# One line moved in a slot of the attention loop: ScalarE's exponentials behind the first half of the group work

## The chip, the cores and the metric

The kernel runs on one core of a Trainium2 chip. The metric is the device time of one execution in microseconds (us); a lower figure is better. The five engines are named as in the profile: PE is TensorE's matmuls, PEld its weight loads, DVE is VectorE, ACT is ScalarE, POOL is GpSimd, and SP is the engine that issues most of the DMAs here.

## What is computed

The input is an image batch of 32 x 128 x 56 x 56 in float32. Layer 0 is a depthwise 7x7 convolution, a layer norm and a mixture of experts with eight experts. Layer 1 works on tokens: there are 32 x 3136 = 100352 of them, each with 128 channels. Its attention is unusual, since it looks across the channels of one head of one token rather than across tokens:

```python
qkv = x @ w_qkv + b_qkv                              # x is the normalised token
q, k, v = (to_heads(t) for t in jnp.split(qkv, 3, axis=-1))   # 8 heads of 16
attn = softmax((q * scale)[..., :, None] * k[..., None, :], axis=-1)   # 16 x 16 per head and token
out = jnp.einsum('bhlij,bhlj->bhli', attn, v)
t = t + (out @ w_proj + b_proj)
```

After it comes a second mixture of experts, in which each of 64 experts takes the tokens of an image that score highest for it. The change lies in the attention stage alone.

## The kernel before

The stages follow one another: convolution, routing and experts (up to 4.31 ms of the span), attention (from about 4.33 to 8.86 ms), and the second mixture with the output. In the attention stage 128 tokens make a tile, seven tiles make a group (`GJ = 7`), and there are 784 tiles (`NT`) and 112 groups (`NG`). Seven groups hold a pair of images.

**A tile's work.** A tile has 128 partitions of 16 x 8 x 16 = 2048 scores. `offsets` (DVE) writes key minus pivot into a buffer `s`; `scores` (POOL) multiplies it by the query in place; `exps` (ACT) takes the exponential in place; `values` (DVE) multiplies by the value vector into `ev`. `sums_s` and `sums_ev` (PE) add up the 16 slices of `s` and of `ev` in PSUM by 16 transposing matmuls each. For every second tile `keys` (PE) computes keys and values of two tiles into the PSUM tile `kv`, `ends` (DVE, two reductions named `kx`) finds the largest and the smallest key of each head, `pivots` (POOL) makes the pivot `c` from them, and `inverse_first` (ACT, two instructions named `r`) and `quotients` (DVE) divide. `s` has five buffers, `ev` three, and `kv` three of two tiles each.

**The slot.** The loop at lines 1479 to 1496 is a software pipeline that is written out by hand. Slot `k` calls each step for another tile: `tile_work(k, back, what)` works on tile `k - back`. So a tile's offsets and scores fall in slot n, its exponentials in slot n + 1, its values and `sums_s` in slot n + 2, and its `sums_ev` in slot n + 3. Each engine is wrapped in `InOrder`, which ties every instruction to the one before it on that engine, so each engine's queue has the order of the text.

**The group's work.** What is done once for seven tiles is cut into pieces with a place in half slots, counted from the group's first tile. `group_work(2 * k)` issues the pieces of the first half of a slot (the even places), and `group_work(2 * k + 1)` those of the second half (the odd places):

```python
(-9, head_turned, first), (-8, head_turned, last),
(-6, head_queries, first), (-5, head_queries, last),
(27, tail_summed, first), (28, tail_summed, last),
(30, tail_rows, first), (31, tail_rows, last),
(39, tail_scale, first), (40, tail_scale, last),
(46, tail_turned, first), (49, tail_turned, last),
```

These six kinds (`takes`) are ACT instructions that empty a PSUM bank which PE had filled a slot or so before: `zT<-p_x`, `q<-p_q`, `t<-pp`, `u<-p_u` with squares `sq<-p_u`, `ls<-p_l` and `lg<-p_g`. Squares of the next groups' tokens (`sq<-tr`), their scaling (`zr`) and `root_first` (`st`) are ACT work too. `choose`, the second mixture's choice of tokens for a pair of images, is a generator that group_work moves on by one step each half slot. All its ACT work, the two passes `pb` over 3136 columns and the scalings `mT<-cm`, falls in even places, since it starts at an even one and its steps lie two or eight half slots apart. The banks for all these transposes and products (`p_x`, `p_q`, `pp`, `p_u`, `p_l`, `p_g`, and `cm` and `acc` of `choose`) come from one ring of three PSUM buffers with the tag `tp`. PE can write to one of them only when ACT or DVE has emptied what it held three allocations before.

Of the kernel before, what the change touches and what calls it, by code (L numbers as in the profile page):

```python
# [25 lines left out]
def conv_attn_hybrid_kernel(  # L26
# [392 lines left out]
    with tc.tile_pool(name="sel", bufs=1) as se, tc.tile_pool(  # L419
# [75 lines left out]
        for e in range(E):  # L495
            k = key[:, e, :]
# [456 lines left out]
    def fetch(i):  # L953

        e = slice(i * Q, (i + 1) * Q)
        fw1s[i] = big.tile([C, Q, FF2], F32, name="fw1", tag="s", bufs=5)
        nc.sync.dma_start(fw1s[i], weight1[e, :C, :].rearrange("e c f -> c e f"))
        fw2s[i] = big.tile([P, Q, NF2, C], F32, name="fw2", tag="ev", bufs=3)
        nc.sync.dma_start(fw2s[i], weight2[e, :FF2, :].rearrange("e (p f) o -> p e f o", f=NF2))

    with tc.tile_pool(name="at_c", bufs=1) as cc, tc.tile_pool(
# [503 lines left out]
        def group_work(place):  # L1465
            for what, of in work.pop(place, ()):
                what(*of)
            if place in choices:
                choosing.append(choose(choices.pop(place)))
            if choosing and next(choosing[0], run) is run:  # L1470
                choosing.pop(0)

        def tile_work(k, back, what, every=1):
            n = k - back
            if 0 <= n < NT and n % every == 0:
                what(n)

        k = -22
        while k < NT or work or choosing or choices:
            tile_work(k, 5, inverse_first, 2)  # L1480
            tile_work(k, -1, ends, 2)
            tile_work(k, 6, quotients, 2)
            tile_work(k, 0, offsets)
            tile_work(k, -1, pivots, 2)
            tile_work(k, 0, scores)
            tile_work(k, 1, exps)
            tile_work(k, -2, keys, 2)
            tile_work(k, 3, sums_ev)
            group_work(2 * k)
            tile_work(k, 2, values)  # L1490
            tile_work(k, 2, sums_s)
            group_work(2 * k + 1)
            if k == NT + 4:
                for i in range(3):
                    fetch(i)
            k += 1
# [121 lines left out]
```

## Time and profile before

| | us |
|---|---|
| median of 3 runs (lowest, highest) | 9425.73 (9423.46, 9436.19) |
| the profiled execution's own time | 9417.63 |
| its span in the profile | 9415.9 |
| attention stage in it, 4340 to 8865 | 4525 |
| busy in that stage: DVE / POOL / PE / ACT | 4368 / 4264 / 4298 / 3689 |

A line of a group of instructions reads: line of the kernel, engine, operation, result and operands with their shapes, and the count; then the busy time in us and the mean of one in ns; then how long the engine had been idle just before these instructions, and what ended most of it. Line 161 stands for all attention instructions, since a helper issues them, so they are told apart by their tiles' names. A line of the waits reads: who waited, for what; us in total, number of waits, longest one. A line of the timeline reads: start in us, duration in us, engine, operation, tiles, count, and in brackets the idle time before it and what ended it.

### The profile page before, as it was taken

The numbers are of one execution on the slowest core, as the hardware profiler recorded it, in microseconds if no ns is written. First come the engines' busy times: TensorE is split into PE (matmuls) and PEld (weight loads), VectorE is DVE, ScalarE is ACT, GpSimd is POOL, SyncE is SP. The second block draws the span as 40 slices with busy tenths as digits, with TensorE's granted clock in tenths as the row PEclk, the third lists the DMA queues.
The fourth block names the chain that finished last, engine by engine and source line by source line (L and its number), as shares of the span: only waits on it lengthen the run. The fifth ranks groups of instructions, "written<-read, shape, count | busy, mean of one in ns | idle before, by whom it ended". The sixth has DMA issues, their size and how long they took to land. (4 is left out here: it accounts for less than half of the span.)

```text
span 9415.9 us, 162622 instructions
## 1 busy us (share of the span) xinstructions
PE 8433.8 (90%) x60648; PEld 6763.7 (72%) x60648; DVE 6437.0 (68%) x10943; ACT 5265.5 (56%) x13401; POOL 6911.7 (73%) x5332
## 2 busy tenths in 40 slices
PE   9998278776999999997999999999999999999878
PEld 3436255554666666666888998988889989888733
DVE  2118889883222222226999999999999999999623
ACT  1118724332333333335888888888888888888600
POOL 0007267777777777778999999999999999999500
PEclk9999699998999999999999999999999999999855
DMA  9996157774444444441000000000000000000299
GB/s 210 215 204 179 34 171 225 209 209 121 69 67 72 65 61 70 70 68 32 25 31 32 30 30 32 25 32 32 28 32 32 25 32 30 30 32 32 65 323 335
DMA packets 996135, 849.73 MB, mean 90 GB/s; under 512 B 525012, under 2 KB 880663, under 8 KB 975858
## 3 DMA queue, kind: packets, MB, share of 16 engines
q1 hardware_dynamic: 470162, 494.25, 18.3%
q0 software_dynamic: 177664, 188.81, 11.3%
q10 hardware_dynamic: 347520, 156.28, 6.1%
q8 instruction: 480, 7.86, 0.3%
q14 instruction: 309, 2.53, 0.1%
HBM read 486.34 MB, written 353.64 MB: 89 GB/s over the span
## 5 line engine op out<-in xcount | busy, mean ns | idle before, releaser
L161 POOL TENSOR_TENSOR s<-s,q 128x2048 f32<-128x2048 f32 x784 | 3601.9, 4605 | 136.1 <-DVE s L161 105.5
L161 ACT ACTIVATE s<-s 128x2048 f32<-128x2048 f32 x784 | 1501.0, 1915 | 687.5 <-POOL s L161 684.0
L161 POOL DMA_INDIRECT t_d<-ys,xe x992 | 1530.6, 1543 | 406.1 <-issue 229.6
L161 DVE TENSOR_TENSOR s<-kv,c 128x2048 f32<-128x2048 f32 x784 | 1788.5, 2281 | 8.0 <-POOL c L161 8.0
L161 DVE TENSOR_TENSOR ev<-s,kv 128x2048 f32<-128x2048 f32 x784 | 1785.7, 2278 | 2.4 <-ACT s L161 2.4
L161 PE MATMUL sm<-ident,ev 128*128 128x128 f32 x12544 | 1531.9, 276 | 45.6 <-DVE ev L161 45.6
L161 PE MATMUL sm<-ident,s 128*128 128x128 f32 x12544 | 1526.3, 276 | 8.4 <-ACT s L161 8.4
L161 PEld LDWEIGHTS sm<-ident,ev 128*128 128x128 f32 x12544 | 1437.4, 144 | 92.9 <-DVE ev L161 50.8
L161 PEld LDWEIGHTS sm<-ident,s 128*128 128x128 f32 x12544 | 1404.8, 143 | 21.0 <-ACT s L161 8.9
L907 ACT ACTIVATE hT<-ph,b1t 128x512 f32<-128x512 f32 (+1 forms) x992 | 679.5, 685 | 1236.4 <-PE ph L903 1220.8
L918 DVE TENSOR_TENSOR ys<-py,b2t 128x512 f32<-128x512 f32 (+1 forms) x248 | 171.6, 692 | 1542.2 <-PE py L913 1445.5
L913 PEld LDWEIGHTS py<-w,hT 128*128 128x128 f32 x7936 | 959.3, 192 | 201.9 <-issue 91.4
L903 PE MATMUL ph<-xeT,w 128*128 128x512 f32 (+1 forms) x1984 | 921.6, 597 | 69.7 <-DVE xeT L899 69.7
L913 PE MATMUL py<-w,hT 128*128 128x128 f32 x7936 | 983.5, 278 | 0.2
L716 POOL DMA_INDIRECT xb_d<-xs,rd x784 | 765.3, 976 | 240.7 <-issue 202.0
L241 PE MATMUL cps<-xin,br 56*64 56x448 f32 x7168 | 684.4, 540 | 11.1 <-DVE br L235 10.7
L903 PEld LDWEIGHTS ph<-xeT,w 128*128 128x128 f32 x1984 | 348.7, 191 | 391.9 <-issue 293.1
L241 PEld LDWEIGHTS cps<-xin,br 56*64 56x64 f32 x7168 | 283.5, 132 | 411.2 <-issue 410.0
L161 PE MATMUL pa<-rw,ct 128*128 128x256 f32 x1568 | 395.4, 391 | 157.4 <-DVE xs L161 157.2
L287 POOL MEMSET code<- 128x64 f32 x1 | 0.2, 151 | 691.7 <-DMA conv_d<-ot 691.7
L161 PEld LDWEIGHTS pa<-rw,ct 128*128 128x128 f32 x1568 | 279.3, 191 | 290.8 <-DVE xs L161 209.2
L161 PE MATMUL kv<-wq,zT 128*128 128x256 f32 x1568 | 417.1, 389 | 54.5 <-DVE ev L161 54.1
(558 smaller groups left out, 13031.2 us busy)
## 6 DMA issues: line engine op xcount, KB each, us to landing
ct<-conv_d SPq DMA_DIRECT2D x192, 448.0 KB
xin<-in_x_dram SPq DMA_DIRECT2D x256, 196.0 KB
conv_d<-ot ACTq DMA_DIRECT2D x512, 98.0 KB
t_d<-xs ACTq DMA_DIRECT2D x112, 448.0 KB
tr<-t_d SPq DMA_DIRECT2D x112, 448.0 KB
to<-t_d SPq DMA_DIRECT2D x32, 1568.0 KB
out_dram<-oo ACTq DMA_DIRECT2D x32, 1568.0 KB
xg<-in_x_dram SPq DMA_DIRECT2D x96, 448.0 KB
```

What stands on the lines that cost most here:

```text
L161: r = getattr(self.engine, name)(*a, **k)
L241: nc.tensor.matmul(pss[r][b * HP : (b + 1) * HP], br[rows, kw, :], xi[rows, b * NB : (b + 1) * NB, kw : kw + W], start=(kw == 0), stop=(kw ...
L287: nc.gpsimd.memset(code, -1.0)
L716: s = nc.gpsimd.indirect_dma_start(out=xb_d, out_offset=bass.IndirectOffsetOnAxis(ap=idx, axis=0), in_=row, in_offset=None, bounds_check=R ...
L903: nc.tensor.matmul(ph[:, :, :rows], w1[:, f * P : (f + 1) * P], xT[:, :, :rows], start=True, stop=True,)
L907: nc.scalar.activation(hT[:, f, :, :rows], ph[:, :, :rows], AF.Gelu, bias=b1t[:, f : f + 1])
L913: nc.tensor.matmul(py[:rows, j, :], hT[:, f, j, :rows], w2[:, f, :], start=(f == 0), stop=(f == NF - 1),)
L918: nc.vector.tensor_tensor(ys[:rows], py[:rows], across(b2t, SB)[:rows], ALU.add)
```

## The change

In a slot's text the call of `exps` moves from ahead of `keys`, `sums_ev` and the first `group_work` to directly behind that `group_work`. Nothing is added or removed, and no buffer changes.

```diff
             tile_work(k, 0, scores)
-            tile_work(k, 1, exps)
             tile_work(k, -2, keys, 2)
             tile_work(k, 3, sums_ev)
             group_work(2 * k)
+            tile_work(k, 1, exps)
             tile_work(k, 2, values)
             tile_work(k, 2, sums_s)
             group_work(2 * k + 1)
```

`exps` is one ACT instruction on a tile. `keys` and `sums_ev` issue PE instructions only.

## The prediction

> **What bounds the kernel now.** I first read the busy time by stage, to see which engine leaves least over. The change touches the attention stage only, so this is the stretch from 4340 to 8865 us (columns: length, then busy time of PE, PEld, DVE, ACT, POOL, the granted clock, DMA):
>
> ```profile
> 4340.00:8865.00 4525.00, 4297.62 (x35604) 4061.00 (x35605) 4368.46 (x3816) 3689.26 (x9137) 4264.25 (x2465) 0.98 0.09 30
> ```
>
> DVE is busy for 4368 of 4525 us, 96.5%. What the stage can give is therefore its 157 us of idle time, unless work is taken off DVE, which this change doesn't do. POOL (94%) and PE (95%) are close behind; ACT has 836 us to spare. The next view is the waits of DVE and of PE in 4550 to 8750 us:
>
> ```profile
> DVE kx L161 <- PE kv L161: 95.7, 106, 4.6
> DVE sm L161 <- ACT r L161: 6.3, 14, 1.4
> ...
> PE kv L161 <- DVE ev L161: 52.0, 25, 3.8
> PE sm L161 <- DVE ev L161: 42.4, 21, 3.5
> PE cm L161 <- ACT lg L161: 32.4, 22, 2.8
> PE cm L161 <- ACT sq L161: 16.8, 14, 1.5
> PE acc L161 <- ACT sq L161: 15.3, 19, 2.1
> PE p_x L161 <- ACT sq L161: 11.1, 10, 1.8
> ```
>
> DVE has one wait of any size: keys that PE delivers late. PE's own waits are of two kinds. It waits for DVE where it is ahead, and for ACT to empty a bank. DVE never waits for the exponentials here. ACT waits a great deal, by the page's row of the exponentials:
>
> ```profile
> L161 ACT ACTIVATE s<-s 128x2048 f32<-128x2048 f32 x784 | 1501.0, 1915 | 687.5 <-POOL s L161 684.0
> ```
>
> In 410 of 784 slots ACT stands in front of a tile whose scores POOL hasn't finished, and the bank-emptying behind it stands too. The third view, the timeline, shows the whole chain once:
>
> ```profile
> 6756.54 1.90 ACT L161 ACTIVATE s<-s 128x2048 f32<-128x2048 f32 x1
> ...
> 6758.34 0.57 ACT L161 COPY u<-p_u 128x512 f32<-128x512 f32 x1
> ...
> 6760.00 1.77 PE L161 MATMUL acc<-mT,u 128*128 128x64 f32 x14 [1.03 <-ACT sq L161]
> ...
> 6763.80 1.03 PE L161 MATMUL kv<-wq,zT 128*128 128x256 f32 x4
> ...
> 6764.87 0.76 DVE L161 TENSOR_REDUCE kx<-kv 128x16 f32<-128x256 f32 x2 [1.31 <-PE kv L161]
> ```
>
> ACT takes 1.9 us for exponentials, only then empties `p_u`; PE waits 1.03 us for that bank, is late with the keys 3.8 us later, and DVE stands for 1.31 us.
>
> **What the Trainium skill says.** "PSUM — Partial Sum Buffer", section Engine vs sequencer instructions: the queues of ScalarE, VectorE and GpSimdE are strict FIFO, and matmuls start in program order. The chain above agrees: the copy doesn't pass the exponential. "Perfetto Trace Analysis", Identifying the Most-Contended Engine, warns that PE's matmul busy share is no measure of its limit; so I take DVE as the bound, and PE's 95% only as a warning (it had 220 us of waits in the stage). The same page, Matmuls, wants PSUM banks rotated so that emptying one overlaps the next; here three banks rotate, and the overlap fails where ACT is held up. "ScalarE: Activation LUTs", What ACT_TABLE_LOAD costs, gives 186 ns + 0.833 ns an element without pointer operands, so an estimate of 1892 ns for 2048; the row has 1915 ns. The new neighbours are the same functions, and ACT's rows of this stage hold no table load.
>
> **The change, part by part.** One ACT instruction per tile, 784 in all, changes places with the ACT instructions of the first half of group work. PE's, DVE's, POOL's and SP's queues keep their order: `exps` issues nothing there, no DMA, and the pieces' DMAs stay in sequence. Those behind even pieces (`t2_d`) may start earlier at a DMA share of 0.09, and POOL's `root_step` waits for `root_first`, an even piece that comes earlier: nothing for either. Busy times stay as they are.
>
> *Removed: waits of PE.* From the timeline of ACT I took start-to-start times of the pieces (a square with its accumulator read 0.26 us, `zr` 0.31, `mT` or `ls` 0.22, `u` 0.45, `t` 0.58, a `pb` 2.9) and summed them by the code's places. The first half averages 1.38 us a slot (nine in ten below 2.74, largest 4.1), the second 1.13. I then traced every PE wait of 0.1 us or more for ACT between 4350 and 8840 us to the ACT instruction that ended it. There are 113 waits with 120.7 us, and 119.6 us of them end with an instruction of the **first half**. All of these gain what stands before them, 1.91 us of exponentials plus the wait for POOL, and nearly every wait is shorter than that: 120 us of PE's idle time would go.
>
> *What of it reaches DVE.* Not all, so I kept a ledger along the timeline: a removed PE wait is a credit; a late `kv` at DVE spends from it, up to the length of DVE's wait; a PE wait for DVE's `ev` sets it to zero, since there PE was early anyhow. Of 96.9 us of late keys, **85.3 us** are covered. Both ends: at most all 96.9 plus the 6 us for `r`, about 103; at least nothing, should PE's own work refill the gap.
>
> *Added: later exponentials.* A tile's exponentials now start at the later of two times: the end of POOL's scores, or the end of ACT's earlier work plus the first half's pieces. Against the trace that is 0.92 us later on average, and 1.19 us if ACT also waits for PE to finish the banks that these pieces read (258 us of such waiting, mostly in time in which POOL wasn't done either). Who waits for exponentials? `values` on DVE and `sums_s` on PE, each a slot later. The distance from the end of `exps` to the start of `values` of the same tile is 3.26 us in the median, 1.69 at the fifth percentile. Subtracting tile by tile, 28 tiles would hold DVE back, by **10.0 us** together. Behind the late exponentials stand the second half's pieces and `r`; they end no later than now except where ACT waits for PE, because the same work has only been turned round in front of a wait.
>
> *Slack that the gain itself uses up.* If DVE runs 85 us faster over 784 slots, it gains 0.11 us a slot, 0.22 us over the two slots from offsets to values, and the distance shrinks by that. The same subtraction with all distances 0.5 us shorter gives 44 us in 104 tiles; between 10 and 44, at 0.22, I take **25 us**. The two bounds are 10 us and, with 1 us less, 110 us in 164 tiles; a stall gives the next tiles their slack back, so such a sum is rather too high.
>
> *Ends of the stage.* The last tile's exponentials come one first half later, at most 2 us, and fetches of expert weights wait for its buffers. The gap in PE's clock is nothing that I can price: the granted clock was 0.98 in this stage and 0.5 to 0.6 behind it, where DMA is 0.78 to 0.95 busy.
>
> *Sum*: -85 + 25 = -60 us. The profiled execution took 9417.63 us (span 9415.9), so a like one would take about 9358. The median of the runs shown is 8.1 us higher; against it the forecast is 9425.7 - 60 = **9366 us**. DVE would then be busy for about 4368 of 4465 us, 98%.
>
> **The rivals.** A measurement of this kernel can tell about 0.2%, 19 us, from no change.
>
> *Nothing comes through.* PE gets its banks earlier but then waits for DVE: `kv` and `sm` wait for `ev` for 94 us already in the view above, 46 times. For it: PE has 95% of work, so a removed wait of 1 us may be filled by a queue that was late anyway. Against it: 85 of 97 us of late keys follow a wait for ACT with no wait for DVE in between. A quarter of the 85 would come through, 21 us, against 10 to 25 us of stalls: -11 to +4, about 9422 us.
>
> *Late exponentials take DVE's time* (the slower side). Place: the slots in which the first half is long (`u` with its squares, `lg` with a root step, each with or without seven `mT`) and in which ACT didn't wait for POOL, so that the exponentials move by the full 2 to 2.7 us. Price: with distances shorter by 1 us it is 110 us, net +25; by 1.5 us 216 us in 242 tiles, net +131. It decides from a shortening of about 0.8 us, where stalls and the 85 us cancel. For it: the median distance after the move is only 2.07 us and the fifth percentile 0.06; POOL starts its scores 1.1 us behind DVE's offsets in the median, and would lag more if DVE ran faster. Against it: POOL needs 4264 us for the stage and DVE 4368, so POOL can follow a DVE without waits, and today POOL waits for `s` from DVE 103 us in 106 slots. At a shortening of 1 us it would be about 9450 us.
>
> *More than forecast.* All late keys vanish and stalls stay at 10 us: -93 us, 9333 us.
>
> That the change doesn't do what it says is no likely case: `InOrder` ties ACT's instructions to the text.
>
> **How the numbers follow.** Forecast 0.60, more than forecast 0.08, nothing through 0.14, late exponentials 0.18. Faster by over 0.2% are the first two, 0.68; within it 0.14; slower by over it 0.18. The forecast's own range is 9340 to 9400. The range that should hold 8 in 10 reaches from 9335, beyond which lies half of the strong case, to 9450, which takes in the quiet case and the mild half of the slow one.
>
> **What would show it.** Right: PE's waits for ACT `lg` and `sq` fall from 120 us to under 30, DVE's wait of `kx` for `kv` from 96 to under 30; ACT's wait for POOL before exponentials falls from 684 to under 350 us; a new wait of DVE `ev` for ACT `s` appears, 2.4 us now, 10 to 45 then; the stage ends about 60 us earlier. The forecast is wrong if DVE's wait for `kv` stays above 60 us (the ledger fails: PE's own work was the cause) or if DVE's wait for ACT's `s` passes 85 us (the distance fails).

## The result, and the profile after

The changed kernel takes 9351.6 us (median of 4 runs, 9348.3 to 9354.7) against 9430.1 us of the kernel before beside it: ratio 0.992, interval 0.9907 to 0.9932, so 78 us less. The two profiled executions took 9348.25 and 9417.63 us, 69 us apart.

By the rows of the tile `s`, the attention stage, taken here from the start of the first offsets to the start of the last tile's values, ran from 4334.8 to 8778.7 us:

```profile
L161 DVE TENSOR_TENSOR s<-kv,c x784: 2269/2279/2293, 4334.8 to 8767.6; 128x2048 f32<-128x2048 f32 x196
...
L161 DVE TENSOR_TENSOR ev<-s,kv x784: 2265/2276/2290, 4345.5 to 8778.7; 128x2048 f32<-128x2048 f32 x196
```

That is 4443.9 us, where the kernel before had 4515.9 (4333.9 to 8849.8): 72 us less. All other time went from 4900.0 to 4902.6 us. So the whole difference lies in this stage. The busy times there (length, PE, PEld, DVE, ACT, POOL, clock, DMA share) are nearly what they were, with a DVE that now stands at 98%:

```profile
4335.00:8779.00 4444.00, 4272.11 (x35499) 4034.58 (x35498) 4360.49 (x3812) 3666.99 (x9107) 4263.00 (x2461) 0.99 0.09 30
```

The waits of DVE, then those of PE, in 4550 to 8750 us, the window of the prediction:

```profile
DVE kx L161 <- PE kv L161: 31.6, 51, 1.2
DVE s L161 <- POOL c L161: 9.8, 17, 0.9
DVE ev L161 <- ACT s L161: 1.0, 4, 0.4
```

```profile
PE kv L161 <- DVE ev L161: 52.7, 25, 3.8
PE sm L161 <- DVE ev L161: 47.6, 26, 3.5
PE p_x L161 <- ACT sq L161: 20.9, 27, 1.5
PE p_g L161 <- ACT zT L161: 10.6, 21, 0.8
PE p_g L161 <- ACT sq L161: 9.2, 14, 1.1
```

Late keys fell from 95.7 to 31.6 us. PE's waits for `lg` are gone, and so are all waits of `cm` and `acc`. What PE still waits for from ACT are other banks. The wait for exponentials that DVE was to pay costs it 1.0 us. The timeline of the tile that the prediction showed (before: 6756.54) reads now:

```profile
6719.17 0.57 ACT L161 COPY u<-p_u 128x512 f32<-128x512 f32 x1
...
6721.23 1.92 ACT L161 ACTIVATE s<-s 128x2048 f32<-128x2048 f32 x1
...
6721.47 1.67 PE L161 MATMUL acc<-mT,u 128*128 128x64 f32 x14
...
6725.17 1.03 PE L161 MATMUL kv<-wq,zT 128*128 128x256 f32 x4
...
6727.22 0.74 DVE L161 TENSOR_REDUCE kx<-kv 128x16 f32<-128x256 f32 x2
```

The copy stands ahead of the exponential, `acc` finds its bank empty, and neither PE nor the reduction has a wait in brackets.

### The profile page after: what moved, and what is told of

Same layout as the page of the kernel before. It is cut to its first block, busy times and chain, and to the rows that moved or that the text cites. A ratio compares the mean times of both kernels' runs of the same rounds, so it can differ in the third digit from the quotient of the medians.

```text
span 9346.5 us, 162593 instructions
## 1 busy us (share of the span) xinstructions
PE 8420.5 (90%) x60648; PEld 6741.5 (72%) x60648; DVE 6429.3 (69%) x10943; ACT 5251.3 (56%) x13401; POOL 6907.4 (74%) x5332
## 5 line engine op out<-in xcount | busy, mean ns | idle before, releaser
L161 DVE TENSOR_TENSOR s<-kv,c 128x2048 f32<-128x2048 f32 x784 | 1787.3, 2280 | 20.3 <-POOL c L161 20.2
```

What stands on the lines that cost most here:

```text
L161: r = getattr(self.engine, name)(*a, **k)
```

## The experiments

**Two theories.** The banks theory: PE gets its PSUM banks sooner, so the keys, so DVE. The fill theory: any ACT work done while ACT waits for POOL is worth time, in proportion. For the kernels e1 to e8 the chip spent some 430 us more outside attention than the one of the runs above (before: 9858 to 9861 us), so times are given as ratios to the kernel before beside them, and stages in us. The stages can be compared all the same: the changed kernel's, repeated there as e5, took 4444.0 us, where the first one took 4443.9. The last two ran where the kernel before takes 9424 us.

**The two parts of the first half.** In e1 only the six kinds of `takes` stay ahead of the exponentials; in e2 only the other ACT work does. The division isn't quite that of banks: the scalings `mT<-cm` empty a bank of the ring too, and they belong to the other work.

```diff
-            group_work(2 * k)
+            takes_work(2 * k)          # e1: `takes`; e2 has rest_work(2 * k) here: squares of tr, zr, roots, choose's ACT steps
             tile_work(k, 1, exps)
+            group_work(2 * k)          # what is left of the half
```

> Only the pieces of the first half that empty a PSUM bank (zT, q, t, u with its squares, ls, lg; about 0.53 us a slot) stay ahead of the exponentials; the other squares, the scaling, the root steps and all of the token choice's ACT work (0.85 us a slot) go behind them again. Banks theory (the gain comes from PE getting its banks sooner, and so the keys): the whole gain is kept, 9340 to 9365 us, PE's waits for ACT stay under 60 us and DVE's wait for kv near 30 us. Fill theory (any ACT work done in the wait for POOL brings gain, in proportion): 0.53 of 1.38, about -30 us, 9400 us.

> The opposite part of the change: of the first half only squares of tr, scaling, root steps and the token choice's ACT work stay ahead of the exponentials (0.85 us a slot); all that empties the banks of the group's own work goes behind them, as before. Banks theory: no gain, 9420 to 9450 us, PE's waits for ACT near 120 us and DVE's wait for kv near 96 us. Fill theory: about -48 us, 9380 us.

Measured: e1 0.9945 (0.9931 to 0.9958), stage 4467.2 us, 49 of the 72 us; e2 1.0006 (0.9998 to 1.0015), stage 4536.0. The two largest of DVE's waits, e1's first and then e2's:

```profile
DVE kx L161 <- PE kv L161: 59.7, 71, 2.1
DVE s L161 <- POOL c L161: 8.8, 10, 1.1
```

```profile
DVE kx L161 <- PE kv L161: 123.9, 120, 3.0
DVE sm L161 <- ACT r L161: 5.5, 9, 0.9
```

The takes carry two thirds, and the larger part of the work (0.85 of 1.38 us a slot) carries nothing by itself: the stage of e2 is even 20 us longer than before. That is against the fill theory. But the banks theory in its simple form was to keep all, and e1 keeps 49 of 72 us. Two of PE's waits in e1 point to what the rest does:

```profile
PE p_g L161 <- ACT zT L161: 18.7, 23, 1.4
PE p_g L161 <- ACT mT L161: 6.6, 7, 1.0
```

The other work, put back behind the exponentials, stands ahead of the slot's second half: the piece of `zT` that these waits end with is an odd one, and the changed kernel has 10.6 us of them. `mT` empties a bank itself and stands behind the exponentials again; the changed kernel has no such wait. So the rest counts where it holds back later banks. In e2 `mT` goes ahead without the takes and finds PE not ready; ACT waits 51 us there for `cm`. So e2 isn't a pure test of the rest either, and the two parts don't add up to the whole (49 and -20 us against 72).

**A bank freed sooner without a change of order.** In e4 the squares of the kernel before read the copy in SBUF, so `p_u` is free after the copy.

```diff
-                squares(ps[:, j - j0, :], ss[:, j : j + 1])
+                squares(u[:, j, :], ss[:, j : j + 1])
```

> The order of the kernel before, with one edit: the squares of a group's rows read the copy u instead of the PSUM bank, so the bank comes free after one copy (0.45 us) instead of after the copy and three or four squares (1.5 us). Of 120 us of PE's waits for ACT 57 us end with a square. Banks theory: each of these waits shrinks by up to 1 us, about 40 to 50 us of them go, the late keys shrink by 25 to 40 us: 9390 to 9408 us. Fill theory: ACT's order and load are unchanged, no gain: 9425 to 9435 us.

Measured 1.0012 (1.0004 to 1.0021), stage 4531.1 us: the banks theory's number failed. PE's waits:

```profile
PE cm L161 <- ACT lg L161: 43.7, 21, 2.8
PE p_x L161 <- ACT lg L161: 34.5, 27, 2.6
PE p_g L161 <- ACT lg L161: 11.9, 7, 2.5
PE acc L161 <- ACT lg L161: 9.0, 7, 1.4
```

The 57 us of waits that ended with a square are gone, but those for `lg` grew from 51 to 99 us; all PE's waits for ACT come to 122 us, where they were 123. The bank that came free a microsecond earlier only brought PE to a later one of the ring: before each of the 62 waits that end with `lg`, exactly one exponential stands on ACT between the last copy `u` and that `lg`. That is the exponential of a later slot, and nothing had moved it. This points to when ACT gets through the pieces as what counts. The edit isn't a pure test, though: it also made ACT's work 42 us longer (last section), and DVE's wait for `r` grew from 9.9 to 20.3 us.

**Further in the same direction.** e3 puts the exponentials behind the second half too; e5 and e6 repeat the changed kernel and e3 side by side.

```diff
-            tile_work(k, 1, exps)
             tile_work(k, 2, values)
             tile_work(k, 2, sums_s)
             group_work(2 * k + 1)
+            tile_work(k, 1, exps)
```

> The exponentials move half a slot further, behind the second half of the group's work too. Banks theory: the first half brings nothing more and no wait of PE was ended by a piece of the second half, so no further gain; the exponentials are about 1.1 us later still, on a distance to values of 2.0 us in the median. With stalls summed over tiles at distances 1.1 us shorter: DVE's wait for ACT s goes from 1 us to 40 to 120 us, 9390 to 9480 us. A theory that there is slack to spare (a late tile costs nothing because DVE's wait is given back): 9345 to 9365 us, wait for ACT s under 20 us.

> The changed kernel itself, beside the two others of this set. Both theories: 0.8% under the kernel before, attention stage near 4444 us.

> The exponentials behind both halves, again, beside the changed kernel. If late keys were nearly all that was left (31.6 us in the changed kernel, 2.6 us with the exponentials behind both halves), it stays 0.15 to 0.3% under the changed kernel, with a stage near 4424 us; if the first comparison was chance, within 0.1% of it.

Measured: e3 0.9903 (0.9888 to 0.9918), stage 4424.1; e6 0.9900 (0.9885 to 0.9915), stage 4424.1; e5 0.9928 (0.9915 to 0.9942), stage 4444.0. The medians of e6 and e5, 9757.5 and 9779.8 us, are 0.23% apart. Two stages each agree within 0.1 us, so the further 20 us are not chance. My expectation of no further gain was wrong. DVE's waits in e6:

```profile
DVE s L161 <- POOL c L161: 20.9, 34, 1.1
DVE ev L161 <- ACT s L161: 9.4, 21, 0.6
DVE kx L161 <- PE kv L161: 2.9, 5, 0.9
```

Late keys are all but gone, and PE's waits for ACT fell from 51 us in the changed kernel to 7 in e3: the banks of the second half had become the next ones to wait for. A tile's exponentials come later again, and DVE waits 9.4 us for them (6.2 in e3), not 40 to 120. This version beats both kernels.

**All takes first.** e7 puts the takes of both halves ahead of the exponentials and everything else behind.

```diff
-            group_work(2 * k)
+            takes_work(2 * k)
+            takes_work(2 * k + 1)
             tile_work(k, 1, exps)
+            group_work(2 * k)
```

> Only the pieces that empty banks go ahead of the exponentials, but those of both halves of the slot (so the odd ones come even earlier than in the changed kernel); squares of tr, scaling, root steps and the token choice's ACT work stay behind. Banks theory: the third of the gain that was missing with the first half's pieces alone (49 of 72 us in the stage) was odd pieces still standing behind other ACT work, so the gain is that of the exponentials behind both halves: stage 4420 to 4435 us, late keys under 10 us, 0.95 to 1.05% under the kernel before. Fill theory: the moved work is 0.53 us of the first half and about the same of the second, less than in the changed kernel: half to three quarters of its gain, 0.4 to 0.65%.

Measured 0.9950 (0.9936 to 0.9963), stage 4460.0: the banks theory's 4420 to 4435 failed. DVE's waits, then ACT's:

```profile
DVE ev L161 <- ACT s L161: 27.7, 33, 2.2
DVE kx L161 <- PE kv L161: 23.4, 28, 1.2
```

```profile
ACT s L161 <- POOL s L161: 376.7, 264, 4.4
ACT ls L161 <- PE p_l L161: 145.2, 102, 3.1
ACT t L161 <- PE pp L161: 134.7, 81, 3.0
```

A take that is moved half a slot forward finds PE not ready, and then ACT stands in front of it with the exponentials behind: 280 us of waits for `p_l` and `pp`, where the changed kernel has 29 for `pp` and none for `p_l`, and DVE waits for exponentials after all. In e3 such waits stand at 212 us and cost DVE 6 us there; why they do less harm in that order I have not separated.

**A whole slot later.** e8 takes `exps` at the changed place for tile k - 2.

```diff
-            tile_work(k, 1, exps)
+            tile_work(k, 2, exps)
```

> The changed kernel with the exponentials a whole slot later (slot k takes tile k - 2), directly ahead of that tile's values in the text. Distances from exps to values are 2.5 us in the mean in the changed kernel and a slot is 5.66 us. Theory of a shrinking distance: DVE now waits for exponentials in most slots, by 0.2 to 0.6 us each, 150 to 450 us in the stage, 1 to 4% slower than the kernel before. Theory that the engines only shift against each other (ACT no longer waits for POOL and runs ahead by as much): waits of DVE for ACT s under 40 us, no slower than the changed kernel by over 0.3%.

Measured 0.9998 (0.9990 to 1.0007), stage 4520.0. Its DVE waits:

```profile
DVE ev L161 <- ACT s L161: 110.4, 153, 2.5
DVE s L161 <- POOL c L161: 9.0, 10, 1.1
```

Both theories missed: there is no late key left at all, and 110 us of waits for exponentials in their place, so the time is that of the kernel before. This is the slower rival's mechanism in the open, at a whole slot's delay.

**More work on PE.** e9 and e10 compute the logits' products twice, in the changed kernel and in e3.

```diff
-                pe.matmul(
+                for _ in range(2):
+                    pe.matmul(
```

> The changed kernel with more work on PE and nothing else: each group's seven products for the logits (p_l) are computed twice over the same output, 0.83 us a group, about 93 us in the stage. PE waits 161 us there, of which 110 us are for DVE and 51 us for ACT. Theory that late keys come from PE being behind for any reason: part of the 93 us falls where PE isn't early, late keys rise from 31.5 us to 60 to 120 us and the stage by as much, to 4470 to 4530 us. Theory that only the wait for a bank makes keys late and PE has room: late keys under 45 us, stage under 4460 us.

> The same additional 93 us of PE work with the exponentials behind both halves, where PE waits 135 us for DVE and 5 us for ACT. PE-behind theory: less than in the changed kernel, since PE is early more often: late keys from 3 us to 15 to 60 us, stage 4435 to 4485 us. Room theory: late keys under 15 us, stage under 4435 us.

Measured 1.0012 (1.0005 to 1.0018) and 1.0016 (1.0009 to 1.0023), stages 4529.3 and 4529.9. The dose was larger than I wrote: the seven products of a group take 1.67 us in the timeline of the changed kernel (14 matmul records), not 0.83, and 3.24 us when doubled; PE's busy time in the stage rose by 134 us in e9. DVE's waits, e9 and then e10:

```profile
DVE kx L161 <- PE kv L161: 123.8, 93, 2.8
DVE s L161 <- POOL c L161: 8.7, 10, 1.1
```

```profile
DVE kx L161 <- PE kv L161: 76.9, 71, 1.9
DVE ev L161 <- ACT s L161: 44.1, 72, 2.0
```

In e9 PE waits only 9 us for ACT, and in e10 not at all, yet the keys are late: they come late as well when it is PE's own work that puts it behind. With PE busy for 97% of the stage both orders end alike, and the gain of the order is gone.

**All kernels in one table.** Of each kernel the stage, DVE's waits from 20 us behind its start (all waits: those of over 0.9 us in total, summed), and the difference, in us. e5 and e6 are repeats and left out:

| kernel | late keys | waits for exponentials | all DVE waits | stage | stage less waits |
|---|---|---|---|---|---|
| before | 96.9 | 2.4 | 112 | 4516 | 4404 |
| changed | 31.6 | 4.1 | 51 | 4444 | 4393 |
| e1 takes of the first half | 59.7 | 0.6 | 69 | 4467 | 4399 |
| e2 the rest of it | 123.9 | 2.5 | 136 | 4536 | 4401 |
| e3 behind both halves | 2.6 | 6.2 | 33 | 4424 | 4391 |
| e4 squares from u | 102.4 | 0.2 | 125 | 4531 | 4406 |
| e7 all takes | 23.4 | 27.7 | 67 | 4460 | 4394 |
| e8 a slot later | 0 | 110.4 | 119 | 4520 | 4401 |
| e9 changed, more PE | 123.8 | 2.0 | 135 | 4529 | 4395 |
| e10 e3, more PE | 76.9 | 44.1 | 130 | 4530 | 4400 |

A stage is an engine's work plus its idle time for any engine, so the sum alone doesn't show that DVE is the bound. What the table adds is that DVE's own part hardly changes: the last column stays within 4391 to 4406 us while the stage moves over 112 us. So the orders differ by DVE's waits, and the columns name which.

## Why the prediction was right, point by point

- **The bound**: right. DVE's own part is the same to 15 us in ten kernels, and where its waits went, the stage became shorter: in e3 DVE is busy for 4357 of 4424 us, 98.5%.
- **Removed waits of PE**: 120 us were to go and under 30 to be left. In the whole stage PE's waits for ACT went from 123 to 51 us. The waits that ended with `lg` went, but others came up behind the second half: 20.5 of the 25 us at `p_x` follow its copy `u`, and the 10.6 us at `p_g` its piece of `zT`. Before the change no wait at these banks ended with a piece of the second half. The ledger took a removed wait as gone for good; here and in e4 it came back in part at another bank.
- **What reaches DVE**: forecast 85.3 us, measured 65.3 us (96.9 to 31.6 in the whole stage). With the exponentials behind both halves late keys are 2.6 us, so what was missing stood behind the second half. The forecast of the wait for `r`, 6 us as an upper end, came in full: 9.9 us to none.
- **Later exponentials**: the mis-sized term. I took 25 us, between 10 and 110. Measured were 1.7 us more of waits for exponentials (2.4 to 4.1). The shift itself came out in size, but by another way. From the end of a tile's offsets to the start of its exponentials it went from 6.04 to 7.04 us in the mean, 1.00 later, where the forecast had 0.92 to 1.19. The working had held POOL's times fixed; yet 0.83 of it is POOL, which starts its scores 1.95 us behind the end of the offsets where it was 1.12, and only 0.17 lies between scores and exponentials (0.31 to 0.48 us). Of the distance to `values` the median fell to 1.98 us, as forecast (2.07), but the fifth percentile only to 0.47 us, not to 0.06. So the shortest distances, from which stalls come, were forecast too short. That POOL's lag spares them, since ACT then does the moved pieces while POOL isn't done, is likely but not separated by a run. That POOL lags because late keys hold DVE back less fits e9 and e10, where late keys are back and the lag is 1.18 and 1.15 us. DVE paid for being ahead in another wait that I hadn't listed, `s` for the pivot `c` from POOL: 2.9 to 15.2 us.
- **The sum**: late keys -65, `r` -10, exponentials +2, pivots +12, together -61 us against -60 forecast. The median of all runs came to 9351.6 us, where 9366 was forecast. That this agrees is luck: 20 us too much credit stand against some 11 us too much for new waits and the 10 us of `r` that the sum left out. The stage fell by 72 us; of the other 11 us, 8 are DVE's busy time in the window (4368 to 4360), and what made that shorter I did not find.
- **What would show it**: the stage ended 72 us earlier, with about 60 named. Three signs missed their figures: PE's waits for `lg` and `sq` fell to 34 us, not under 30, late keys to 31.6, not under 30, and DVE's wait for exponentials is 4.1 us, not 10 to 45. ACT's wait for POOL ahead of exponentials was to fall from 684 to under 350 us and stayed at 682: ACT meets POOL later, since POOL lags more; instead ACT's waits for `sm` fell from 80 to 11 us. That sign was wrong as a test.
- **The slower rival**: its mechanism exists. A whole slot of delay brought 110 us of stalls and no gain. The distance in the mean was 3.67 us before and 2.48 in the changed kernel; with the exponentials behind both halves it is 2.01 us, 1.7 less than before, and stalls are still 6 us, while a whole slot later it is 1.39, 2.3 less. So the point from which stalls outweigh the gain lies between a shortening of 1.7 and one of 2.3 us. The prediction put it at 0.8 us beyond the move's own 0.92 to 1.19, so at 1.7 to 2.0 in all, which the runs don't refute. But for half a microsecond beyond the move it had 44 us of stalls, and e3, about as far, has 6.

## What to carry to other kernels

Where engines run in lockstep through queues in program order, look for a long instruction that waits for one engine while short ones behind it hold a resource of another; give the short ones the place ahead of it, up to the point where they wait themselves. Sum the waits of the engine with the least idle time, see whether its own work stays the same, and judge each order by that sum: here the rest was the same to 15 us. Distances read from a trace with the other engines' times held fixed overstated here what the later instruction costs (10 to 25 us against 2), though their median came out right; the producers shift as well. And a removed wait for a buffer may come back at a later buffer of the ring.

## What was not expected of the hardware

My expectation for e4 had ACT's load unchanged, but reading the squares' source from SBUF instead of PSUM costs time. From the start of one square to that of the next the timeline has 249 ns in the median before and 293 ns in e4, 44 ns more, and the squares `sq<-tr`, which read SBUF in both, take 292 ns. ACT's busy time in the stage rose from 3681 to 3723 us. "Perfetto Trace Analysis", Optimizing Scalar/DVE Operations, gives about 93 ns of access for ScalarE on SBUF and 51 ns on PSUM, a difference of 42 ns: the trace agrees.
